# Moving the load of Wo and one activation-table load in a graph-attention and mixture-of-experts layer

## The chip, the cores and the metric

The kernel runs on one core of one Trainium2 chip. A core has five engines that run their own instruction lists: TensorE (PE in the profile; its weight loads are shown apart as PEld), VectorE (DVE), ScalarE (ACT), GpSimd (POOL) and SyncE (SP). They meet only through semaphores. Transfers are issued from the lists of SP, ACT and POOL and carried out by 16 shared DMA engines; an instruction that issues a transfer waits in its engine's list like any other, and what stands behind it waits too. The metric is the time of one launch in microseconds (us), lower is better. The time before the change is 2276.78 us, the median of five runs (2266.71, 2267.69, 2276.78, 2277.61 and 2291.95 us).

## The reference: what is computed

One layer over N = 4096 nodes with 512 features, in two halves, each with a layer norm ahead of it and a residual around it.

- **Attention over a sparse graph.** For 8 heads of width 64, q, k and v are projected from the normed x by Wqs, Wks, Wvs. A node attends only to its neighbours in `adj` (4096 x 4096, zeros and ones, fewer than one in a hundred of them ones, and far more of those at low node numbers) and to itself:

```python
scores = jnp.einsum('hqk,hmk->hqm', q, k) * kd ** (-0.5)
scores = scores + IDENTITY_BIAS * eye - MASK_VAL * (1.0 - adj)
att = jax.nn.softmax(scores, axis=-1)
return jnp.einsum('hqm,hmk,hko->qo', att, v, Wo)
```

- **Mixture of experts.** Each node goes to the two of 8 experts with the highest logits; an expert is 512 -> 512 -> 512 with a gelu, and the two results are added with softmax weights.

## The kernel before, in words

`_fast` is one long function, and the order of the instructions on each engine is the order in which it is written (a manual schedule); the framework adds the waits. It has three stages.

**Stage one: projections and lists (0 to about 456 us).** For 32 tiles of 128 nodes the kernel norms and transposes x, multiplies it by Wk and Wv, and stores a row of keys, values and packed adjacency words per node in the DRAM table `kv_d`. Queries are projected by `project_q(b, p)` for blocks of 512 nodes, in `NP` = 4 pieces p of 128 columns: four matmuls (L600), then a scaled copy by ACT (L605) and a store to `q_d` issued by ACT (L606). Meanwhile other instructions build, for every tile of queries, index lists `idx` of the neighbours that it has to fetch. The stage ends with the four pieces of the last block:

```python
for p in range(NP):
    project_q(NT // TPB - 1, p)
while jobs:
    step()
```

ACT also computes square roots in this stage (L385, norms), with its own activation table.

**Stage two: attention (about 456 to 1720 us).** The work is cut into steps, and steps are grouped in pairs ("duos"). A step takes one or two sets of 128 neighbours, fetched from `kv_d` into one of 24 slots of a ring in SBUF: a tile's own rows by SP (L702), the others by an indirect DMA that POOL issues (L707), whose instruction is visible on POOL as DMA_INDIRECT. For each step, `turn` transposes the keys on PE (L734, tile `pkT`) and has ACT copy them to SBUF (L736, tile `kT`); `scores` multiplies them with the queries (L771, tile `ps`) and has ACT take the exponential (L778, tile `pr`); DVE masks it by the adjacency bits (L784, or L782 for own rows); `values` multiplies by the values (L799). After a query tile's last step its sums are divided, transposed and multiplied by Wo (`project`, L844), which is the only reader of the tile `wo`; the route to the experts follows in the same loop.

**Around the change.** Between the stages stand these lines, in this order (L1118 to L1174, helpers left out):

```python
nc.vector.tensor_copy(wg32[:, :, :E], wg)
tick = small.tile([1, 1], F32, bufs=1, name="tick")
wo = mid.tile([P, NP, D], F32, name="wo")
nc.scalar.dma_start(out=wo, in_=Wo...)        # L1121, 1024 KB, on ACT's queue
...
issue(3, -1)
duo(turn, 0)
nc.gpsimd.tensor_copy(tick, steps[duos[0][0]]["kT"][0][:1, 0, :1])   # L1170
issue(AHEAD, -1)
duo(scores, 0)
duo(turn, 1)
duo(turn, 2)
n = 0
```

`issue(k, n)` issues the fetches of the duos below k. Duos 0 to 2 need one fetch by SP and seven by POOL. The copy `tick` on POOL reads one element of the first `kT`, so no later fetch is issued before that copy is done. `AHEAD` is 5, and inside the loop that follows `issue` goes on as far as the ring has slots, so in POOL's list sixteen more fetches stand behind `tick` ahead of the first one that needs a slot back.

The tile `wo` lies in memory that stage one used. So its load waits, at the head of what ACT has left, for the last stores of stage one, that of the last piece of queries among them. ACT's list at the joint of the stages is: copy of query piece 2 and its store; copy of piece 3 and its store; the load of `wo`; two copies `kT` of duo 0; a table load for the exponential; two exponentials of duo 0; four copies `kT` of duos 1 and 2; exponentials of duo 1; and so on.

**Stage three: experts (about 1720 us to the end)** is not touched by the change.

Of the kernel before, what the change touches and what calls it, by code (L numbers as in the profile page):

```python
# [9 lines left out]
F32 = mybir.dt.float32  # L10
# [4 lines left out]
AF = mybir.ActivationFunctionType  # L15
# [5 lines left out]
P = 128  # L21
# [49 lines left out]
def fast(tc, dram, flag, x, adj, Wks, Wqs, Wvs, Wo, Wg, bg, W1, b1, W2, b2, out):  # L71
    with ExitStack() as ctx:
        _fast(ctx, tc, dram, flag, x, adj, Wks, Wqs, Wvs, Wo, Wg, bg, W1, b1, W2, b2, out)


def _fast(ctx, tc, dram, flag, x, adj, Wks, Wqs, Wvs, Wo, Wg, bg, W1, b1, W2, b2, out):
    nc = tc.nc
    N, D = x.shape
# [7 lines left out]
    NP = H * KD // P  # L86
# [29 lines left out]
    eps = const.tile([P, 1], F32, name="eps")  # L116
    nc.vector.memset(eps, EPS)
    bits = const.tile([P, NW, 16], U16, name="bits")
    for k in range(16):
# [4 lines left out]
        out=below, in_=below, pattern=[[1, P]], compare_op=ALU.is_gt, fill=0.0,  # L124
# [209 lines left out]
    with ExitStack() as s1:  # L334
# [7 lines left out]
        work = s1.enter_context(tc.tile_pool(name="p1", bufs=2))  # L342
# [205 lines left out]
        for h in range(NHC):  # L548
# [4 lines left out]
            g, c = divmod(h, NH)  # L553
# [36 lines left out]
        def step():  # L590
            nonlocal slot
            for f in jobs.pop(slot, []):
                f()
            slot += 1

        def project_q(b, p):
            pq = ps_m.tile([P, TB], F32, tag="mm", name=f"pq_{b}_{p}")
            for c in range(DC):
                step()
                nc.tensor.matmul(  # L600
                    pq, w["q"][:, c, ts(p, P)], xTs[b][:, c, :],
                    start=(c == 0), stop=(c == DC - 1),
                )
            qT = work.tile([P, TB], F32, tag="qT", bufs=3, name=f"qT_{b}_{p}")
            nc.scalar.mul(qT, pq, KD ** -0.5)  # L605
            nc.scalar.dma_start(out=q_d[:, p, ts(b, TB)], in_=qT)  # L606

        for i in range(NT):
            b, t = divmod(i, TPB)
            kvr = kvrs[i % 2]  # L610
            for k, n in enumerate(("k", "v")):
# [15 lines left out]
                out=kv_d[1 + i * P : 1 + (i + 1) * P, :HV], in_=kvr.bitcast(I32)  # L627
# [2 lines left out]
                project_q(b - 1, t)  # L630
        for p in range(NP):
            project_q(NT // TPB - 1, p)
        while jobs:
            step()

# [9 lines left out]
    with ExitStack() as s2:  # L645
# [3 lines left out]
        mid = s2.enter_context(tc.tile_pool(name="mid", bufs=1, side="right"))  # L649
# [223 lines left out]
        def route(g, n):  # L873
# [243 lines left out]
        AHEAD = 5  # L1117
        nc.vector.tensor_copy(wg32[:, :, :E], wg)  # L1118
        tick = small.tile([1, 1], F32, bufs=1, name="tick")
        wo = mid.tile([P, NP, D], F32, name="wo")  # L1120
        nc.scalar.dma_start(  # L1121
            out=wo, in_=Wo.rearrange("h k o -> (h k) o").rearrange("(c p) o -> p c o", p=P)
        )
        issued = 0

        def issue(upto, n):
# [35 lines left out]
        def duo(f, n):  # L1162
            if n < S:
                for s in duos[n]:
                    f(s)
# [6 lines left out]
        duo(scores, 0)  # L1172
        duo(turn, 1)
        duo(turn, 2)  # L1174
        n = 0
        while n < S or any(k >= n for k in later):
            duo(scores, n + 1)
# [86 lines left out]
    with ExitStack() as s4:  # L1264
        work = s4.enter_context(tc.tile_pool(name="p4", bufs=2))
# [793 lines left out]
```

## Time and profile before

| | before |
|---|---|
| median of five runs | 2276.78 us |
| profiled execution, its own time | 2272.34 us |
| its span, first to last instruction | 2270.6 us |
| mean granted TensorE clock | 0.941 of full |
| PE busy | 91% of the span |
| ACT, DVE, POOL busy | 35%, 43%, 25% |
| moved by DMA | 462 MB, mean 203 GB/s |

All of the profile comes from the one profiled execution. A line of the timeline reads: start, duration, engine, line of the kernel, operation, written tile <- read tiles, shapes, how many instructions were merged, and in brackets how long the engine sat idle before it and what ended that wait. "issue" means that the engine waited for nothing that the profile shows. ACTq marks instructions of ACT's list that only issue or wait. A matmul in float32 with these shapes leaves two records. A row of the table by windows reads: stretch, its length, busy time (and records) of PE, PEld, DVE, ACT and POOL, the granted TensorE clock as a share of full speed, the mean busy share of the 16 DMA engines, and what they moved in GB/s.

### The profile page before, as it was taken

What the parts mean: (1) busy time and instruction counts of PE and PEld (TensorE: products, weight loads), DVE (VectorE), ACT (ScalarE), POOL (GpSimd) and SP (SyncE); (2) the same over time, 40 slices, a digit from 0 to 9 for tenths busy, and PEclk for the clock granted to TensorE, in tenths of its full rate; (3) what the DMA queues carried; (4) which work ended last, traced back from release to release, by engine and by line L of the source; (5) the groups of instructions that cost most, each with busy time, mean ns of one, the idle gap of its engine ahead of it and who ended that gap; (6) DMA issues with size and microseconds to landing.
All of it is one profiled execution on the core that took longest, in us unless ns stands there. A gap on an engine that the chain in (4) does not pass through costs nothing. (4 is left out here: it accounts for less than half of the span.)

```text
span 2270.6 us, 59938 instructions
## 1 busy us (share of the span) xinstructions
PE 2056.2 (91%) x25581; PEld 1352.7 (60%) x25581; DVE 971.4 (43%) x2519; ACT 793.5 (35%) x1166; POOL 561.9 (25%) x716
## 2 busy tenths in 40 slices
PE   9899999979999978979979889788887999999997
PEld 4344444468777757767757667576665444444443
DVE  3456655425434434434434445245354333333332
ACT  3233333135444524524534345243431222222221
POOL 2000000143333342343242331423211122222221
PEclk9999999989999989979979889798898999999999
DMA  9778773486677666766667584866686455455532
GB/s 373 255 263 263 261 262 123 156 296 225 222 234 250 227 225 215 228 223 220 221 221 232 175 273 157 274 206 192 220 291 234 106 109 116 107 123 133 110 72 44
DMA packets 193602, 462.00 MB, mean 203 GB/s; under 512 B 30384, under 2 KB 46768, under 8 KB 193200
## 3 DMA queue, kind: packets, MB, share of 16 engines
q0 software_dynamic: 66784, 248.65, 36.1%
q1 hardware_dynamic: 102096, 178.04, 23.7%
q10 hardware_dynamic: 24448, 31.38, 4.1%
q8 instruction: 206, 3.38, 0.6%
q14 instruction: 68, 0.56, 0.1%
HBM read 385.37 MB, written 72.64 MB: 202 GB/s over the span
## 5 line engine op out<-in xcount | busy, mean ns | idle before, releaser
L707 POOL DMA_INDIRECT ring<-kv_d,idx x361 | 355.4, 985 | 1084.2 <-issue 471.1
L771 PE MATMUL ps<-q,kT 64*64 64x64 f32 (+1 forms) x10224 | 398.5, 245 | 106.7 <-issue 93.1
L778 ACT ACTIVATE pr<-ps 128x1024 f32<-128x1024 f32 x270 | 272.4, 1025 | 565.7 <-PE ps L771 431.3
L784 DVE SCALAR_TENSOR_TENSOR pr<-t,pr 128x1024 f32<-128x1024 uint16 x238 | 285.7, 1223 | 402.5 <-ACT pr L778 341.0
L771 PEld LDWEIGHTS ps<-q,kT 64*64 64x64 f32 (+1 forms) x10224 | 327.2, 153 | 186.2 <-issue 163.7
L799 PE MATMUL o<-ring,pr 128*64 128x65 f32 x8640 | 309.2, 228 | 32.3 <-issue 32.3
L799 PEld LDWEIGHTS o<-ring,pr 128*64 128x64 f32 x8640 | 281.5, 141 | 66.0 <-issue 62.8
L734 PE MATMUL pkT<-ident,ring 128*128 128x128 f32 x1572 | 226.8, 295 | 21.1 <-issue 13.2
L1402 PE MATMUL ph<-ring,xT 128*128 (+1 forms) x528 | 238.2, 594 | 0.8 <-ACT xT L1364 0.8
L734 PEld LDWEIGHTS pkT<-ident,ring 128*128 128x128 f32 x1572 | 186.2, 150 | 43.8 <-issue 20.6
L736 ACT COPY kT<-pkT 128x512 f32<-128x512 f32 (+1 forms) x270 | 199.3, 787 | 26.1 <-PE pkT L734 12.5
L1458 POOL DMA_INDIRECT out_dram<-y,r x66 | 101.9, 1544 | 371.1 <-ACT y L1453 284.2
L1431 PE MATMUL py_e<-ring,hT 128*128 (+1 forms) x396 | 182.3, 596 | 1.6 <-ACT hT L1424 1.6
L1402 PEld LDWEIGHTS ph<-ring,xT 128*128 128x128 f32 (+1 forms) x528 | 91.3, 183 | 99.8 <-issue 98.7
L1453 ACT ACTIVATE y<-y,wt 128x512 f32<-128x512 f32 x66 | 47.6, 722 | 269.8 <-DVE y L1449 230.0
L615 PE MATMUL pv<-wv,xT 128*128 128x512 f32 x256 | 130.0, 603 | 0.0
L844 PE MATMUL py<-wo,oT 128*128 128x512 f32 x256 | 125.2, 634 | 2.6 <-ACT part L937 1.8
L615 PE MATMUL pk<-wk,xT 128*128 128x512 f32 x256 | 125.7, 610 | 0.7 <-ACT xT L409 0.7
L600 PE MATMUL pq<-xT,wq 128*128 128x512 f32 x256 | 123.1, 603 | 0.0
L1407 DVE COPY h<-ph 128x512 f32<-128x512 f32 x66 | 45.7, 692 | 169.9 <-PE ph L1402 169.9
L1431 PEld LDWEIGHTS py_e<-ring,hT 128*128 128x128 f32 (+1 forms) x396 | 67.2, 183 | 76.0 <-issue 74.1
L1073 POOL DMA_INDIRECT xs_d<-x,slot_i x58 | 63.8, 1100 | 173.7 <-DVE x L1069 57.1
(281 smaller groups left out, 1905.9 us busy)
## 6 DMA issues: line engine op xcount, KB each, us to landing
adj<-in_adj_dram SPq DMA_DIRECT2D x64, 1024.0 KB
wo<-in_L_ffn_W_dram SPq DMA_DIRECT2D x72, 256.0 KB
kv_d<-kvr ACTq DMA_DIRECT2D x32, 516.0 KB
ring<-kv_d SPq DMA_DIRECT2D x32, 516.0 KB
r<-xs_d SPq DMA_DIRECT2D x57, 258.0 KB
ring<-in_L_ffn_W_dram SPq DMA_DIRECT2D x56, 256.0 KB
xt<-in_x_dram SPq DMA_DIRECT2D x32, 256.0 KB
q_d<-qT ACTq DMA_DIRECT2D x32, 256.0 KB
```

Of the source, the lines that this page charges most:

```text
L600: nc.tensor.matmul(pq, w["q"][:, c, ts(p, P)], xTs[b][:, c, :], start=(c == 0), stop=(c == DC - 1),)
L615: nc.tensor.matmul(pk, xTs[b][:, c, ts(t, P)], w[n][:, c, :], start=(c == 0), stop=(c == DC - 1),)
L707: nc.gpsimd.indirect_dma_start(out=g, out_offset=None, in_=kv_d, in_offset=bass.IndirectOffsetOnAxis(ap=idx[i // GL][:, i % GL, a : a + 1] ...
L734: nc.tensor.transpose(pk[:, x * NP + p, :], g[:, ts(p, P)], ident)
L736: nc.scalar.copy(kT[:, : nk * NP], pk[:, : nk * NP])
L771: nc.tensor.matmul(ps[c : c + nk, r, p * P + x * nq : p * P + (x + 1) * nq], kT[r * KD : (r + 1) * KD, p, c : c + nk], q[r * KD : (r + 1) ...
L778: nc.scalar.activation(pr.rearrange("p h q -> p (h q)"), ps.rearrange("p r f -> p (r f)"), AF.Exp)
L784: nc.vector.scalar_tensor_tensor(pr, st["t"].unsqueeze(1).to_broadcast([P, H, P]), 0.0, pr, op0=ALU.is_gt, op1=ALU.mult,)
L799: nc.tensor.matmul(o[c * HALF : (c + 1) * HALF, h // NP, (h % NP) * VW : (h % NP + 1) * VW], pr[:, hd * NP + p, c * HALF : (c + 1) * HALF] ...
L844: nc.tensor.matmul(hold["py"], hold["oT"][:, c, :], wo[:, c, :], start=(c == 0), stop=(c == NP - 1),)
L1402: nc.tensor.matmul(ph[a], xTs[b][:, c, a], w, start=(c == 0), stop=(c == DC - 1), skip_group_check=b >= FULL,)
L1431: nc.tensor.matmul(py[a], hTs[b][:, c, a], w, start=(c == 0), stop=(c == HC - 1), skip_group_check=b >= FULL,)
```

## The change

Two edits. The tile `wo` and its load are written after the scores of duo 0 and the transposes of duos 1 and 2, in place of ahead of everything in stage two. And after piece 2 of the last block of queries ACT takes the exponential of one column of a constant into a tile of its own, `one`, that nothing reads; the table load for the exponential then stands there.

```diff
         for p in range(NP):
             project_q(NT // TPB - 1, p)
+            if p == NP - 2:
+                one = work.tile([P, 1], F32, tag="one", name="one")
+                nc.scalar.activation(one, eps, AF.Exp)
         while jobs:
             step()
...
         tick = small.tile([1, 1], F32, bufs=1, name="tick")
-        wo = mid.tile([P, NP, D], F32, name="wo")
-        nc.scalar.dma_start(
-            out=wo, in_=Wo.rearrange("h k o -> (h k) o").rearrange("(c p) o -> p c o", p=P)
-        )
         issued = 0
...
         duo(scores, 0)
         duo(turn, 1)
         duo(turn, 2)
+        wo = mid.tile([P, NP, D], F32, name="wo")
+        nc.scalar.dma_start(
+            out=wo, in_=Wo.rearrange("h k o -> (h k) o").rearrange("(c p) o -> p c o", p=P)
+        )
         n = 0
```

In the changed kernel ACT's list at the joint is: copy of query piece 2 and its store; the table load and the exponential `one`; copy of piece 3 and its store; two copies `kT` of duo 0; two exponentials of duo 0; four copies `kT` of duos 1 and 2; the load of `wo`; exponentials of duo 1. The lists of PE, DVE, POOL and SP are the same as before, with the same waits.

## The prediction

> **What bounds the kernel now.** I read the page's first part, then busy times by stage, then the timelines of ACT, PE and POOL around the joint of stages one and two, the only place that the diff touches.
>
> ```profile
> PE 2056.2 (91%) x25581; PEld 1352.7 (60%) x25581; DVE 971.4 (43%) x2519; ACT 793.5 (35%) x1166; POOL 561.9 (25%) x716
> ```
>
> ```profile
> 0.00:455.00 455.00, 436.82 (x2474) 204.79 (x2474) 236.74 (x721) 139.40 (x304) 19.61 (x126) 0.99 0.72 245
> 455.00:488.00 33.00, 19.85 (x187) 16.23 (x188) 7.11 (x16) 11.24 (x14) 16.36 (x17) 0.70 0.90 346
> 488.00:1720.00 1232.00, 1072.10 (x21135) 877.83 (x21134) 542.05 (x1326) 519.78 (x648) 409.31 (x496) 0.91 0.68 226
> ```
>
> PE is the busy engine of every long stage (96% and 87% above). The joint, 455 to 488 us, is the exception: PE is busy for 19.85 of 33 us, at a mean clock of 0.70. ACT's timeline shows why it begins late:
>
> ```profile
> 451.94 0.33 ACTq L606 DMA_DIRECT2D q_d<-qT  x1
> 455.27 0.60 ACT L605 ACTIVATE qT<-pq 128x512 f32<-128x512 f32 x1 [3.36 <-PE pq L600]
> 455.90 0.33 ACTq L606 DMA_DIRECT2D q_d<-qT  x1
> 459.14 0.39 ACTq L1121 DMA_DIRECT2D wo<-in_L_gnn_Wo_dram  x1
> 459.62 1.07 ACT L736 COPY kT<-pkT 128x512 f32<-128x512 f32 x2 [3.76 <-DMA q_d<-qT]
> 460.72 1.28 ACT L778 ACT_TABLE_LOAD   x1
> 462.01 1.02 ACT L778 ACTIVATE pr<-ps 128x1024 f32<-128x1024 f32 x1
> 463.38 1.02 ACT L778 ACTIVATE pr<-ps 128x1024 f32<-128x1024 f32 x1 [0.35 <-PE ps L771]
> ```
>
> The last store of queries is issued at 455.90. The load of Wo behind it can be issued only when that store has landed, at 459.14, and the first copies of turned keys stand behind the load. PE and POOL wait for those copies:
>
> ```profile
> 455.97 1.07 PE L734 MATMUL pkT<-ident,ring 128*128 128x128 f32 x8 [0.73 <-issue]
> 460.26 3.07 PE L771 MATMUL ps<-q,kT 64*128 64x128 f32 x32 [3.23 <-ACT kT L736]
> 463.27 3.43 PE L734 MATMUL pkT<-ident,ring 128*128 128x128 f32 x24
> 466.62 1.08 PE L771 MATMUL ps<-q,kT 64*64 64x64 f32 x38
> ...
> 483.76 2.72 PE L734 MATMUL pkT<-ident,ring 128*128 128x128 f32 x12 [0.64 <-issue]
> ```
>
> ```profile
> 460.27 0.18 POOL L1170 COPY tick<-kT 1x1 f32<-1x1 f32 x1 [11.51 <-ACT kT L736]
> 460.61 0.96 POOL L707 DMA_INDIRECT ring<-kv_d,idx  x1 [0.16 <-issue]
> ```
>
> PE turned the keys at 455.97 and stood still for 3.23 us. Then comes a second, larger loss that the change does not address: from 467.5 to 483.1 PE gets through only the last 42 of the 80 records of duo 1's scores, in bursts of one to six with gaps marked "issue". These 15.6 us lie inside POOL's burst of sixteen fetches behind `tick`, 460.6 to 481.4, with the DMA engines full:
>
> ```profile
> 458.00:460.00 2.00, 0.00 (x0) 0.00 (x0) 0.00 (x0) 0.38 (x1) 0.00 (x0) 1.00 0.02 6
> 462.00:464.00 2.00, 2.00 (x18) 1.77 (x15) 0.93 (x1) 1.64 (x2) 1.70 (x2) 0.50 1.10 398
> 470.00:484.00 14.00, 6.05 (x29) 4.28 (x30) 0.00 (x0) 0.09 (x1) 8.62 (x10) 0.55 1.02 406
> ```
>
> The same sight returns in every later place where POOL issues back to back: around 810 us PE's `values` trickle from 809.7 while POOL issues from 805.2, and run again at 823.7, when POOL pauses. So I take it that this stretch ends with POOL's burst, whatever PE has left.
>
> **The change, part by part.** (1) The load leaves the head of ACT's list. Nothing then stands between the store at 455.90 and the first `kT`, whose waits are on PE and DVE alone. Its four transposes, the first half of the x8 row, end at 456.60; the copy then starts at about 456.65 in place of 459.62: 2.97 us earlier. `tick`, the burst and the first scores each hang on that copy by fixed steps (460.27 minus 459.62 is 0.65; 460.26 minus 459.62 is 0.64), so all move by 2.97.
>
> (2) PE's clock. The granted share falls to 0.77 and 0.50 in 460 to 464, behind the gap, and the first scores take 3.07 us; the same 32 records take 2.06 us later (at 504.31). Without the gap up to 1.0 us goes, and some 0.2 of the transposes: 0 to 1.2 us more. But it is regained ahead of the trickle, which ends with POOL, so at 2.7 records per us (42 in 15.6) 1.2 us earlier buys 3 records, 0.1 us at full speed. I take 0.1.
>
> (3) The table load, 1.28 us, and the new exponential (nearest row: the one-column square root of L385, 0.29) take 1.57 us between 452.27, when the store's issue ends, and 455.27, when ACT next has work: a hole of 3.00, spare 1.43. Cost nothing; with no cover it would hold the last queries by 1.57. What it frees at 460.72 is at most 0.7 us: at full clock the first half of duo 0's scores is done 1.03 after 457.29, at 458.3, and a load left behind the two `kT` copies would end at 459.0. PE covers that with 24 transposes (3.4 us) before it needs ACT again. I take 0, keep 0 to 0.7.
>
> (4) The load's new place. Its issue, 0.39, follows the four copies of duos 1 and 2 (464.97 plus 2.91, less about 3: near 465), when the stores that it waits for have landed (459.1). Behind it on ACT stand duo 1's exponentials, due after 480: ACT is idle for 16.04 us there. No engine waits; SP and POOL keep their lists. Its data, 1 MB, now fall among the fetches, 2.6 us at 406 GB/s; before, they went ahead of them (the engines moved 218 and 398 GB/s from 460 to 464). The fetches behind it feed duo 3 and later, which PE takes up only at the end of the trickle, and POOL issues every 1.24 us unhindered: cost 0 to 0.6, taken 0. The first reader, L844, comes at 571.1 us, 107 us later.
>
> Sum: 2.97 + 0.1 + 0 + 0 = **3.1 us** off, bounds 2.4 (2.97 less 0.6) to 4.9 (2.97 + 1.2 + 0.7). After the joint no row is tied to the clock on the wall, so the shift reaches the end. The profiled execution took 2272.34 us (2270.6 of span and 1.74 around it): it would take 2269.2. That execution lies 4.4 below the median of the five, 2276.78; a median is what will be compared, so I forecast 2276.78 - 3.1 = **2273.7**.
>
> Two rules of the Trainium skill are weighed here. "ScalarE: Activation LUTs", under "What ACT_TABLE_LOAD costs", adds a drain of about 1.38 us to a load, 2.66 us in all; with 0.29 that would fill 2.95 of the 3.00 us hole, and any slip would delay the last queries. In the row above the next exponential starts 0.01 us after the load, so this trace shows no such drain; by either the sum stays 3.1. "TensorE: Matmul & The Clock Gate", in "Part 1: The HAM clock gate", halves the clock after an idle window of about 3.4 us; read as a gap of that length, the 3.23 us here would cost no clock, and the sum would be 3.0. The trace did halve it.
>
> **The rivals.** *Nothing is kept.* The trickle could end at its old time, if what ends it is the drained transfers and not POOL: the 1 MB that no longer goes ahead, and a store that is still landing, may eat the lead of 2.97. For it: DMA is at 1.02 until 484. Against it: the engines do next to nothing in 458 to 460 (6 GB/s), which the change fills. Time 2276.8.
>
> *Slower.* PE enters the trickle earlier. Before, it ran 94 record pairs of weight load and matmul at full rate from 460.26 to 467.5, out of what its sequencer held when POOL began; 3.23 us of standstill preceded. If less is at hand without that pause, more is left at the burst's end. Worst: the trickle from the start, 20.8 us of burst at 2.7 a us, 56 records of the 136 (32 + 24 + 80) that were done before; 80 remain, 3.0 us at full clock and 6.0 at half. Against 3.0 gained that is 0 to 3 lost: 2280. It turns slower once more than 40 records (3.0 us at the half clock) are left. For it: nothing shows how many were held. Against it: 809.7 is 4.5 us into POOL's burst with no pause ahead of it.
>
> *Larger gain.* PE's supply lasts a little longer and the scores of duo 1 are out before the trickle; then the 12 transposes and 64 records of `values` that now take 483.76 to 489.32 also go early: 3.1 + 5.6, time 2268. For it: the scores start 0.9 us earlier relative to the burst at full clock. Against it: the trickle seems to hang on the count of instructions, which is unchanged.
>
> **How the numbers follow.** Forecast 0.60, nothing kept 0.16, slower 0.12, larger gain 0.12. All lie within 1% (22.8 us), about what a measurement of this kernel can tell from no change: its five runs span 25.2 us, so even a median may stray some 7 us. The range takes in the rivals and part of that: 2268 - 6 = 2262 to 2280 + 5 = 2285. Faster or slower by over 1% has only this scatter behind it: 0.03 each, 0.94 the same.
>
> **What would show it.** Right: the first `kT` directly behind the last store's issue, PE's gap before the first scores under 0.5 us, clock at 1.00 in them, `tick` near 457.3, the table load near 452.3, POOL's sixteen fetches ended by 478.5, the second transposes near 480.7. Wrong: a wait on the last store again, fewer than 38 records before the trickle, or another length of it.

## The result and the profile after

The changed kernel takes 2274.48 us (median of 52 runs), the kernel before 2276.52 us (94 runs): ratio **0.999, 95% interval 0.998 to 1.0001**, or 2.3 us less with an interval from 4.6 less to 0.2 more (the medians differ by 2.0). No difference that the measurement can tell. Ratios leave out runs over 1.5% above the fastest of their kernel, two of the 52 here. The profiled execution after took 2274.75 us (span 2273.0, clock 0.938), 2.4 us more than the one before, although the joint went as intended. ACT's timeline after, in the columns explained above (line numbers are 3 higher than before):

```profile
452.67 1.28 ACT L635 ACT_TABLE_LOAD   x1 [0.39 <-ACT qT L605]
453.96 0.20 ACT L635 ACTIVATE one<-eps 128x1 f32<-128x1 f32 x1
455.64 0.60 ACT L605 ACTIVATE qT<-pq 128x512 f32<-128x512 f32 x1 [1.47 <-PE pq L600]
456.26 0.33 ACTq L606 DMA_DIRECT2D q_d<-qT  x1
457.00 1.07 ACT L739 COPY kT<-pkT 128x512 f32<-128x512 f32 x2 [0.77 <-PE pkT L737]
459.21 1.02 ACT L781 ACTIVATE pr<-ps 128x1024 f32<-128x1024 f32 x1 [1.14 <-PE ps L774]
461.40 1.02 ACT L781 ACTIVATE pr<-ps 128x1024 f32<-128x1024 f32 x1 [1.16 <-PE pkT L737]
...
464.29 0.39 ACTq L1175 DMA_DIRECT2D wo<-in_L_gnn_Wo_dram  x1
...
475.45 1.02 ACT L781 ACTIVATE pr<-ps 128x1024 f32<-128x1024 f32 x1 [10.22 <-remote]
481.86 1.02 ACT L781 ACTIVATE pr<-ps 128x1024 f32<-128x1024 f32 x1 [5.38 <-remote]
```

The table load and the exponential stand in the old hole, and the last copy of queries still waits 1.47 us for PE behind them: nothing was delayed. The first `kT` waits for PE alone. From the start of the last copy of queries it starts after 1.36 us in place of 4.35. PE's and POOL's timelines after:

```profile
456.33 1.07 PE L737 MATMUL pkT<-ident,ring 128*128 128x128 f32 x8 [0.73 <-issue]
457.64 2.06 PE L774 MATMUL ps<-q,kT 64*128 64x128 f32 x32 [0.24 <-ACT kT L739]
459.62 1.53 PE L737 MATMUL pkT<-ident,ring 128*128 128x128 f32 x12
462.48 1.56 PE L737 MATMUL pkT<-ident,ring 128*128 128x128 f32 x12 [1.32 <-ACT pr L781]
463.97 1.04 PE L774 MATMUL ps<-q,kT 64*64 64x64 f32 x52
...
466.79 3.02 PE L774 MATMUL ps<-q,kT 64*64 64x64 f32 x20 [0.37 <-issue]
470.43 1.23 PE L737 MATMUL pkT<-ident,ring 128*128 128x128 f32 x5 [0.62 <-issue]
...
476.53 1.11 PE L737 MATMUL pkT<-ident,ring 128*128 128x128 f32 x4 [3.87 <-issue]
...
481.78 3.17 PE L802 MATMUL o<-ring,pr 128*64 128x65 f32 x53 [0.44 <-issue]
```

```profile
457.65 0.18 POOL L1169 COPY tick<-kT 1x1 f32<-1x1 f32 x1 [8.58 <-ACT kT L739]
457.99 0.96 POOL L710 DMA_INDIRECT ring<-kv_d,idx  x1 [0.16 <-issue]
...
478.84 0.94 POOL L710 DMA_INDIRECT ring<-kv_d,idx  x1 [0.30 <-issue]
```

The page's first line and the row of the joint in the table by windows:

```profile
PE 2056.0 (90%) x25581; PEld 1356.3 (60%) x25581; DVE 972.0 (43%) x2519; ACT 794.0 (35%) x1167; POOL 563.2 (25%) x716
```

```profile
452.00:485.00 33.00, 22.17 (x233) 17.00 (x236) 8.53 (x22) 11.73 (x16) 18.86 (x18) 0.73 0.94 358
```

PE's busy time is as before. At the joint, PE is busy for 22.17 of 33 us in place of 19.85 (the stretch is laid 3 us earlier, as the work is). PE's standstill of 3.23 us is 0.24, and the first scores take 2.06 us in place of 3.07. New is a standstill of 1.32 us after the first twelve transposes. The stretch in which PE gets through only a few records at a time, with gaps marked "issue" (the trickle), is still there, from 465 until 481.78. POOL's run of sixteen fetches, 457.99 to 479.78, begins before it and ends 2.0 us ahead of its end (2.4 us before: 481.4 and 483.76).

In this stretch PE's rows don't tell when its results are ready. By them the scores of duo 1 end at 467.1 and 469.8, but ACT is released to their exponentials only at 475.45 and 481.86. "remote" means that no recorded end lies close to the release: the semaphore that PE raises rose 8.3 and 12.0 us after the recorded ends. Away from POOL's runs it rises 0.02 us after them (median in this trace).

Where did the gain go afterwards? Measured at the products with Wo (L847 after, L844 before), in time from the start of the span, the profile after minus that before is -1.85 us at the first product, -5.80 at the second, +2.58 at the fourth, -2.80 at the 18th and +2.20 at the last: it wanders inside stage two. Stage three takes the same time in both. So the two profiled executions can't show a difference of 3 us at the end; only many runs can, and those put it at 2.3 with the interval above.

### The profile page after: what moved, and what is told of

It is laid out like the page before. It is cut to its first block, busy times and chain, and to the rows that moved or that the text cites. A ratio compares the mean times of both kernels' runs of the same rounds, so it can differ in the third digit from the quotient of the medians.

```text
span 2273.0 us, 59939 instructions
## 1 busy us (share of the span) xinstructions
PE 2056.0 (90%) x25581; PEld 1356.3 (60%) x25581; DVE 972.0 (43%) x2519; ACT 794.0 (35%) x1167; POOL 563.2 (25%) x716
## 5 line engine op out<-in xcount | busy, mean ns | idle before, releaser
L774 PE MATMUL ps<-q,kT 64*64 64x64 f32 (+1 forms) x10224 | 393.5, 246 | 92.0 <-issue 81.7
L847 PE MATMUL py<-wo,oT 128*128 128x512 f32 x256 | 123.5, 627 | 2.9 <-ACT part L940 1.7
L1076 POOL DMA_INDIRECT xs_d<-x,slot_i x58 | 65.2, 1125 | 175.3 <-DVE x L1072 57.3
```

The source lines that it names most:

```text
L774: nc.tensor.matmul(ps[c : c + nk, r, p * P + x * nq : p * P + (x + 1) * nq], kT[r * KD : (r + 1) * KD, p, c : c + nk], q[r * KD : (r + 1) ...
L847: nc.tensor.matmul(hold["py"], hold["oT"][:, c, :], wo[:, c, :], start=(c == 0), stop=(c == NP - 1),)
```

## The experiments

A comparison with a time is made with runs of the kernel before on the same chip, and a ratio has its 95% interval. In the landmarks, time is counted from the start of the last copy of queries (the L605 row near 455.5). None of the kernels leaves work out. Those with an addition are named.

### The two edits alone

Without the exponential (the other edit kept):

```diff
-            if p == NP - 2:
-                one = work.tile([P, 1], F32, tag="one", name="one")
-                nc.scalar.activation(one, eps, AF.Exp)
```

> The changed kernel without the early exponential: only the load of Wo is moved. My theory (the wait at the head of ACT's list was the whole cost, the table load is free): the first copy of turned keys starts under 1 us after the last store of queries is issued, PE's gap before the first scores is under 0.5 us, and the table load stands behind the two copies and delays the first exponential by at most 0.7 us, which PE covers with its 24 transposes. Rival (the table load was part of the gain): the first exponential comes over 1 us later than in the changed kernel, relative to the first copy, and PE waits for it.

One run, 2286.69 us, beside a median before of 2293.60 on that chip (2277.13 to 2302.57). Its ACT timeline:

```profile
458.02 1.07 ACT L736 COPY kT<-pkT 128x512 f32<-128x512 f32 x2 [0.77 <-PE pkT L734]
459.11 1.28 ACT L778 ACT_TABLE_LOAD   x1
460.40 1.03 ACT L778 ACTIVATE pr<-ps 128x1024 f32<-128x1024 f32 x1
461.79 1.02 ACT L778 ACTIVATE pr<-ps 128x1024 f32<-128x1024 f32 x1 [0.36 <-PE pkT L734]
```

The first `kT` is at +1.36 us as in the changed kernel. The table load stands behind it again, and the first exponential starts at +3.75, against +3.57 and +3.21 in two executions of the changed kernel. The second one, released by PE, starts at +5.14, against +5.76 and +5.77. In this trace the early exponential frees nothing that PE needs.

The kernel before with the exponential, Wo still ahead:

```diff
+            if p == NP - 2:
+                one = work.tile([P, 1], F32, tag="one", name="one")
+                nc.scalar.activation(one, eps, AF.Exp)
```

> The kernel before with the early exponential alone. My theory: the first copy of turned keys still waits for the landing of the last store of queries, about 3.7 us on ACT, and PE stands still about 3.2 us before the first scores; the clock still falls behind the gap. Only the 1.28 us table load is gone from between the copies and the first exponential, and that exponential then waits for PE instead, at most 0.3 us earlier. Rival (the table load was a real part): the joint is shorter by about 1.3 us.

One run, 2291.59 us. Its ACT timeline:

```profile
460.55 0.39 ACTq L1124 DMA_DIRECT2D wo<-in_L_gnn_Wo_dram  x1
461.03 1.07 ACT L739 COPY kT<-pkT 128x512 f32<-128x512 f32 x2 [2.97 <-DMA q_d<-qT]
```

The wait on the store is there, so the load of Wo is what holds the first `kT`. But `kT` starts at +3.56, not at +4.35: here the load is issued 2.45 us after the issue of the last store, in the profile before 3.24 us after it. The price of the wait is not a constant; in two executions the first `kT` came 2.99 and 2.20 us behind the +1.36 without it.

### Is a delay at the joint carried to the end?

The changed kernel with 48 exponentials of 128 x 256 on ACT ahead of the first `kT`; they write junk into a tile that is filled later:

```diff
         AHEAD = 5
+        for _ in range(48):
+            nc.scalar.activation(
+                inverses.rearrange("p i h -> p (i h)"), blank[:, : NT * H], AF.Exp
+            )
```

> The changed kernel with 48 exponentials of 128x256 on ACT between the last store of queries and the first copy of turned keys, so that the first copy comes some 15 to 22 us later (the trace gives the exact delay). My theory: no row behind the joint is tied to absolute time, so the whole delay reaches the end, within the scatter of stage two: time of the changed kernel plus the delay. Rival (a shift at the joint is absorbed by slack in stage two): less than half of the delay is left at the end.

The first `kT` starts at +22.36 us, 21.0 later than in the changed kernel. ACT's timeline of this run:

```profile
457.62 21.45 ACT L1122 ACTIVATE inverses<-blank 128x256 f32<-128x256 f32 x48 [0.40 <-ACT qT L605]
478.98 1.05 ACT L739 COPY kT<-pkT 128x512 f32<-128x512 f32 x2
```

Time 2308.64 us, ratio to before 1.0083 (1.0048 to 1.0118), which is 19.0 us (11.0 to 27.1) over the kernel before; 21.0 less the 2.3 that the changed kernel gains is 18.7. So more than half of the delay reaches the end, and within the interval all of it; at the first product with Wo (+137.25) all of it is there. That a gain of 2 to 3 us at the joint reaches the end in the same way is likely, but not shown: the interval is wider than the gain.

### The changed kernel again

No edit; it shows how far two executions of one program differ.

> The changed kernel itself, beside the others of this group on one chip, as their baseline. My theory: 1 to 4 us under the kernel before; first copy of turned keys 1.4 us after the last copy of queries starts, values of duo 0 ended 28 to 32 us after it (before: 34.1). Rival (nothing is kept): same time as before to within 1 us.

2274.11 us (12 runs), ratio 1.0002 (0.9978 to 1.0026). Its joint agrees with the profile after up to the trickle and then differs: by PE's rows the scores of duo 1 end at +27.54 us in place of +14.17. By ACT's, the last exponential of duo 1 starts at +27.59 in place of +26.22. Side by side with the two kernels and the two single edits, in us from the last copy of queries:

| run | Wo moved | first kT | scores of duo 1 end by PE's rows | ACT's last exponential of duo 1 | values of duo 0 end | values of duo 7 end | first product with Wo |
|---|---|---|---|---|---|---|---|
| before | no | 4.35 | 27.86 | 29.56 | 34.12 | 75.24 | 115.81 |
| exponential only | no | 3.56 | 22.00 | 28.80 | 33.40 | 77.17 | 117.89 |
| after | yes | 1.36 | 14.17 | 26.22 | 29.32 | 73.02 | 113.60 |
| after again | yes | 1.36 | 27.54 | 27.59 | 31.73 | 74.53 | 115.07 |
| Wo only | yes | 1.36 | 22.78 | 26.79 | 31.73 | 74.04 | 114.73 |

The row of ACT before, where both exponentials of duo 1 are merged:

```profile
483.91 1.94 ACT L778 ACTIVATE pr<-ps 128x1024 f32<-128x1024 f32 x2 [16.04 <-PE ps L771]
```

PE's rows put the end of duo 1's scores 13 us apart in two executions of the same program, ACT's row puts it 1.4 us apart, and both are out of the joint within 1.5 us of each other. ACT's last exponential of duo 1 starts 2.1 to 5.1 us behind the end of POOL's run in all five. The first product with Wo comes at 114.5 in the mean of the three with Wo moved and at 116.9 in that of the two without: 2.4 us, the size of the wait removed (2.2 to 3.0). With three and two executions that differ by 1.5 and 2.1 us among themselves, this is weak evidence by itself.

### What the trickle is: POOL's run of fetches, or full DMA engines?

The changed kernel with a gate on POOL, for the first eight passes of the loop: the copy `tick` reads the first `kT` of duo n + 3 before the next fetches are issued.

```diff
         AHEAD = 5
+        GATED = 8
...
+                if n < GATED:
+                    nc.gpsimd.tensor_copy(
+                        tick, steps[duos[n + 3][0]]["kT"][0][:1, 0, :1]
+                    )
                 issue(n + 1 + AHEAD, n)
```

> The changed kernel with a one-element copy on POOL, reading the newest turned keys, ahead of each of the next eight groups of fetches, so that POOL issues two fetches per duo in place of sixteen back to back. My theory (PE trickles because POOL issues fetches back to back): the stretch of bursts with gaps marked issue between about 465 and 482 us shrinks to a few us behind the first five fetches, the values of duo 0 end near 473 in place of 485, and the time falls by about 10 us, to 2264. Rival (PE's supply stalls there for another reason, or the later fetches then come late): the stretch stays over 10 us, or PE waits for fetched rows instead, and the time is within 3 us of the changed kernel.

2287.84 us, ratio 0.9978 (0.9952 to 1.0003). The 10 us expected did not come. But the trickle at the joint is gone: the scores of duo 1 end at +11.55, ACT's last exponential of duo 1 starts at +11.60, and the values of duo 7 end at +58.12, 14.9 us ahead of the changed kernel. When the gate is lifted POOL catches up, with sixteen fetches on end from 515.65 to 537.45, and PE trickles there. PE's timeline of this run:

```profile
463.53 0.75 PE L774 MATMUL ps<-q,kT 64*64 64x64 f32 x28
464.71 1.91 PE L774 MATMUL ps<-q,kT 64*64 64x64 f32 x52 [0.43 <-issue]
466.56 1.53 PE L737 MATMUL pkT<-ident,ring 128*128 128x128 f32 x12
468.02 2.09 PE L802 MATMUL o<-ring,pr 128*64 128x65 f32 x64
...
531.49 0.82 PE L774 MATMUL ps<-q,kT 64*128 64x128 f32 x4 [0.61 <-issue]
```

The first product with Wo comes at +117.06, 3.5 us later than in the changed kernel. The trickle goes where POOL's run goes.

The other way round, the changed kernel without the holding copy, so that POOL issues all 23 fetches from 440.73 to 471.04, over the end of stage one:

```diff
         duo(turn, 0)
-        nc.gpsimd.tensor_copy(tick, steps[duos[0][0]]["kT"][0][:1, 0, :1])
         issue(AHEAD, -1)
```

> The changed kernel without the copy on POOL that holds the sixteen fetches until the first turned keys are copied: POOL issues all 23 from 440 us on, beside the last projections of queries, and is done near 470 in place of 480. My theory (the trickle lasts as long as POOL's run of fetches, and the projections, with few long matmuls, do not suffer from it): the trickle ends near 471 to 473, the values of duo 0 end 18 to 22 us after the last copy of queries starts in place of 29, and the time falls by 7 to 10 us against the changed kernel. Rival (PE has to lose a fixed amount, or the first seven fetches and the last stores of queries then land late): first transposes come later by several us, or the trickle covers the same count of records, and the time stays within 3 us.

2275.87 us (median of all 12), ratio 0.9981 (0.9951 to 1.0011): the 7 to 10 us expected did not come. PE's timeline:

```profile
452.15 3.60 PE L600 MATMUL pq<-xT,wq 128*128 128x512 f32 x8
471.76 1.94 PE L737 MATMUL pkT<-ident,ring 128*128 128x128 f32 x8 [16.02 <-issue]
473.89 3.13 PE L774 MATMUL ps<-q,kT 64*128 64x128 f32 x32 [0.19 <-ACT kT L739]
```

Now PE's rows show one block of 16.02 us ahead of the first transposes, marked "issue" like the gaps of the trickle, and it ends 0.72 us behind POOL's last fetch. The last projections of queries, recorded as done by 455.75, reach ACT late as well: its last two copies of queries start at 460.51 and 471.07, both "remote", in place of about 452 and 456. Then PE goes on without a trickle; its first values end at 485.5 us, as in the profile after (485.0). Moved earlier, the loss is as large as before.

Full DMA engines without POOL: the gate again, and behind `tick` (by a copy of 4 bytes that waits for it) SP copies 8.4 MB from DRAM to DRAM.

```diff
+        full = dram.tile([1, GL * P, N], F32, name="full_d")
...
+            nc.sync.dma_start(
+                out=full[k], in_=adj[k * GL * P : (k + 1) * GL * P, :N]
+            )
         issue(AHEAD, -1)
...
```

> The gated kernel with one copy of 8.4 MB from DRAM to DRAM, issued by SP when POOL's holding copy is done, so that the transfer engines are full behind the first scores while POOL issues few fetches. My theory (POOL's run of fetches makes the trickle, full transfer engines alone do not): PE runs duos 1 to 4 without long runs of gaps marked issue, though it may wait for rows that land late, and the busy share of the transfer engines is above 0.9 there. Rival (full transfer engines make the trickle): bursts of one to six records with gaps marked issue over 10 us or more, with POOL idle in between.

One run, 2286.43 us. Its table by windows, then PE's timeline:

```profile
464.00:470.00 6.00, 3.21 (x87) 2.61 (x84) 3.57 (x9) 4.00 (x5) 1.15 (x1) 0.96 0.98 371
470.00:482.00 12.00, 0.07 (x1) 0.10 (x2) 0.26 (x2) 0.00 (x0) 0.00 (x0) 0.50 1.11 373
```

```profile
465.72 1.90 PE L774 MATMUL ps<-q,kT 64*64 64x64 f32 x51 [0.41 <-issue]
481.93 1.09 PE L737 MATMUL pkT<-ident,ring 128*128 128x128 f32 x4 [14.31 <-DMA ring<-kv_d,idx]
```

With the engines at 0.98 and POOL at one fetch, duo 1's scores run at full speed; then PE waits 14.31 us for fetched rows, and the wait is named. So here full engines give a named wait on data, and a run of POOL's fetches gives short bursts of PE with gaps named "issue". PE had only some 3 us of work in that stretch, but two other traces say the same of the fetched rows themselves: without the holding copy the engines are at 1.02 from 472 to 476 us, still with POOL's rows but POOL no longer issuing, and PE is busy for 3.81 of the 4 us; before, they are at 1.01 from 484 to 486, and PE is busy throughout.

How POOL's issuing reaches into PE stays open. A late fetch of PE's instructions is not what the traces show: they list the transfers of instructions, and PE goes on without one. In the profile before none starts between 463.98 and 484.63 us, and PE goes on at 483.76; without the holding copy none starts between 444.05 and 477.53, and PE goes on at 471.76.

The gate through all of stage two:

```diff
         AHEAD = 5
+        GATED = S - 3
...
+                if n < GATED:
+                    nc.gpsimd.tensor_copy(
+                        tick, steps[duos[n + 3][0]]["kT"][0][:1, 0, :1]
+                    )
                 issue(n + 1 + AHEAD, n)
```

> The one-element copies on POOL of the gated kernel, kept up through the whole of stage two, so that the fetches are never more than about three duos ahead. In the gated kernel the trickle went from 464-482 us, and a run of 17 fetches came back at 515-537 us when the gate was lifted. My theory (a run of fetches back to back is what costs, and every gate lift or long wait of POOL makes one): without a lift there is no second trickle at 523-538, the first product with Wo comes 12 to 15 us earlier than in the changed kernel, and the time falls by 5 to 20 us, unless POOL's waits for its scatters then leave PE waiting for rows. Rival (the deep lead is needed): PE waits for fetched rows at each scatter, several us at every group of four tiles, and the time is above the kernel before.

2322.16 us, ratio 1.0216 (1.0165 to 1.0267): slower, where 5 to 20 us less were expected. It has no run of eight fetches before 1725 us, yet PE's busy time rose to 2095.5 us from 2056.0, and its waits on `pr` (PE `pkT` <- ACT `pr`) to 20.3 us from 10.2. Why its matmuls take longer was not settled. So doing away with the runs is not enough by itself, and what follows is only that a short lead, held by a gate, is no cure.

### A lead that grows, and where its gain came from

If the loss comes with runs, the lead can be built up slowly: in pass n POOL issues the fetches of the duos below n + 6 + n/3, over the first 18 duos, with the gate; behind them the lead stays at n + 12.

```diff
+                if n < 18:
+                    nc.gpsimd.tensor_copy(
+                        tick, steps[duos[n + 3][0]]["kT"][0][:1, 0, :1]
+                    )
-                issue(n + 1 + AHEAD, n)
+                issue(n + 1 + AHEAD + min(n, 18) // 3, n)
```

> As after, but for the first 18 duos POOL issues only as far ahead as a lead that grows by one duo every three duos: in each of these loop passes POOL's copy `tick` first reads the first kT of duo n+3 and POOL then issues the fetches of the duos below n + 6 + n/3 (whole number), so that neither sixteen fetches at the start nor a catching-up burst later stand back to back. Nothing is left out. Theory 1 (PE loses time only where POOL issues in a long run, and the loss is more than one fetch costs when it stands alone): no trickle at 464 to 482 us, none near 515 to 540, first L844 product about 104 to 110 us after the last copy of queries in place of 113.6 to 115.1, time 5 to 10 us below that of the changed kernel, ratio to the kernel before 0.994 to 0.997. Theory 2 (each fetch costs PE about the same wherever it stands, so the loss is only spread): first L844 at 113 to 117, ratio 0.998 to 1.001. Theory 3 (the smaller lead lets late rows through, as when the gate stood through all of stage two): named waits of PE on fetched rows or of POOL on kT grow, time up to 15 us above.

The same over 12 duos, with n/2:

```diff
+                if n < 12:
+                    nc.gpsimd.tensor_copy(
+                        tick, steps[duos[n + 3][0]]["kT"][0][:1, 0, :1]
+                    )
-                issue(n + 1 + AHEAD, n)
+                issue(n + 1 + AHEAD + min(n, 12) // 2, n)
```

> The same with a lead that grows by one duo every two duos over the first 12. Theory 1: the lead is rebuilt at twice the pace at which one fetch per step is needed, so a milder trickle than in the changed kernel is left: first L844 about 107 to 112 us after the last copy of queries, time 2 to 7 us below the changed kernel, ratio 0.995 to 0.998. Theory 2: 113 to 117, ratio 0.998 to 1.001. Theory 3: up to 10 us above, less than with the slower ramp.

2258.35 us, ratio **0.9906** (0.9874 to 0.9938), and 2261.72 us, ratio **0.9914** (0.9881 to 0.9947). Both are faster than the kernel before, and by more than the largest gain expected of them. But not by the mechanism expected: the first product with Wo comes at +110.21 us in the slow ramp (expected 104 to 110) and at +120.91 in the quick one (expected 107 to 112), which is later than in the changed kernel. Nor did the ramps do away with the runs: POOL still issues fifteen fetches on end from 520.79 to 543.65 in the slow one and eleven from 534.07 to 549.97 in the quick one. Most of the gain must lie behind that product. In the profile after, POOL's timeline at one of six like places:

```profile
1262.00 0.09 POOL L1075 MEMSET tick<- 1x1 f32 x1
1283.19 3.07 POOL L1076 DMA_INDIRECT xs_d<-x,slot_i  x1 [21.11 <-DVE x L1072]
...
1287.87 0.98 POOL L710 DMA_INDIRECT ring<-kv_d,idx  x1 [0.30 <-issue]
```

L1076 scatters rows of x to the experts, and POOL's list holds fetches behind it. POOL waits 21.11 us for the scatter's data and then issues eighteen transfers, scatters and fetches, in a run, and PE trickles: it is busy for all 21 us from 1262 to 1283, while POOL waits, and for 13.08 of the 25 us from 1283 to 1308. The same stands at 808, 998, 1147, 1418 and 1580 us, with waits of 11.6 to 21.1 us. With a lead of n + 12, nine, ten, seven, nine, eight and four more fetches stand ahead of the first scatter of each group, POOL has work until the data are there, and all six waits are gone in both ramps (at most 1.9 us is left of one). That made two explanations, told apart by doing either half alone.

The deep lead without gate and ramp:

```diff
-                issue(n + 1 + AHEAD, n)
+                issue(n + 1 + AHEAD + 6, n)
```

> As after, but in the loop POOL's list goes on to the fetches of the duos below n + 12 in place of n + 6, as far as the ring has slots; no added copies on POOL, the run of sixteen at the start stays. Nothing is left out. It undoes the first half of the kernel with the slow ramp and keeps its second. Theory A (that kernel gained 23 us over the changed one, by its trace, not at the start but because nine, ten, seven, nine, eight and four more fetches then stand ahead of the first scatter of each group of tiles, so that POOL no longer waits 12 to 21 us at that scatter with fetches behind it and then issues 13 to 18 of them in a run): the trickle at 464 to 482 stays, first L844 product 113.6 to 116 us after the last copy of queries, the six waits at scatters gone, time 14 to 22 us below the kernel before, ratio 0.990 to 0.994. Theory B (the gain came from the ramp at the start): ratio 0.998 to 1.001, the waits at the scatters still there or gone without effect.

2270.28 us, ratio **0.9924** (0.9897 to 0.9951), with the trickle at the joint kept (first product with Wo at +114.17). POOL's timeline of this kernel where the changed one waited 21.11 us:

```profile
1300.57 0.94 POOL L710 DMA_INDIRECT ring<-kv_d,idx  x1 [4.55 <-DVE pr L787]
1301.52 0.09 POOL L1075 MEMSET tick<- 1x1 f32 x1
1301.82 1.01 POOL L1076 DMA_INDIRECT xs_d<-x,slot_i  x1 [0.21 <-POOL tick L1075]
```

The groups of POOL by line (busy us, mean ns of one, idle us ahead), the scatters after and then here; the idle time falls by 92.9 us, and the six waits were 96.0 together:

```profile
L1076 POOL DMA_INDIRECT xs_d<-x,slot_i x58 | 65.2, 1125 | 175.3 <-DVE x L1072 57.3 <-DVE var L884 56.1 <-ACT pr L781 26.8
```

```profile
L1076 POOL DMA_INDIRECT xs_d<-x,slot_i x58 | 62.5, 1077 | 82.4 <-DVE var L884 55.3 <-DVE place L1001 11.5 <-issue 10.4
```

The table by windows at three of the six places, of after and then of this kernel:

```profile
1140.00:1174.00 34.00, 19.82 (x362) 16.62 (x359) 8.64 (x29) 8.75 (x10) 18.07 (x24) 0.70 0.68 234
1278.00:1312.00 34.00, 20.07 (x332) 16.12 (x332) 8.70 (x27) 8.44 (x11) 20.49 (x26) 0.67 0.64 226
1410.00:1446.00 36.00, 21.25 (x377) 17.34 (x374) 9.98 (x35) 8.62 (x11) 20.51 (x25) 0.73 0.68 231
```

```profile
1140.00:1174.00 34.00, 30.12 (x717) 24.38 (x716) 18.73 (x57) 14.44 (x18) 15.58 (x15) 0.99 0.75 250
1278.00:1312.00 34.00, 30.28 (x592) 24.70 (x591) 17.70 (x48) 14.59 (x19) 10.80 (x14) 0.95 0.68 226
1410.00:1446.00 36.00, 32.80 (x692) 26.69 (x692) 18.46 (x52) 14.93 (x19) 15.05 (x20) 1.00 0.79 270
```

In these stretches PE gets through almost twice as many records, at a clock of 0.95 to 1.00 in place of 0.67 to 0.73: the clock is low where PE trickles. Over the whole trace PE's gaps named "issue" ahead of scores, values and transposes of keys fall from 141.2 to 120.6 us. A deep lead also brings every row in earlier; a kernel that moves only the fetches at the six scatters was not tried, so the share of the waits in the gain is argued from these traces. The other half, the ramp and then the old lead of n + 6:

```diff
+                if n < 18:
+                    nc.gpsimd.tensor_copy(
+                        tick, steps[duos[n + 3][0]]["kT"][0][:1, 0, :1]
+                    )
-                issue(n + 1 + AHEAD, n)
+                issue(n + 1 + AHEAD + (n // 3 if n < 18 else 0), n)
```

> The other half: the slow ramp of the first 18 duos with its copies on POOL, and after it the lead of n + 6 again as in the changed kernel, so that each scatter stands behind the same fetches as there. Nothing is left out. Theory A: no trickle at 464 to 482, first L844 product about 110 us after the last copy of queries, 3 to 5 us ahead of the changed kernel, and no more than that at the end, since the six waits and runs at the scatters are back: ratio 0.996 to 0.999. Theory B: ratio 0.990 to 0.993 as with the whole of it.

2285.87 us, ratio 0.9992 (0.9965 to 1.0019). The trickle at the joint is gone (values of duo 7 end at +59.14), but the lead of 13.9 us is lost by the first product with Wo (+113.83, expected about 110), and the six waits are back. (In this kernel, too, POOL still issues twelve fetches on end, from 516.88 to 534.06.) So the gain of the ramps is that of the deep lead. The traces say it again in two halves, cut where the 4321st of the 8640 records of `values` starts, counted from the last copy of queries:

| run | first half, us | from there to the end, us |
|---|---|---|
| before | 594.5 | 1220.8 |
| after | 592.6 | 1224.8 |
| after again | 597.9 | 1219.9 |
| ramp, then old lead | 588.1 | 1226.9 |
| deep lead | 607.6 | 1204.0 |
| slow ramp, deep lead | 592.1 | 1201.8 |
| quick ramp, deep lead | 610.2 | 1195.0 |

The second half is 1195 to 1204 us with the deep lead and 1220 to 1227 without it. In the first half the two kernels that build the deep lead quickly are 10 to 18 us longer than the changed kernel, and the slow ramp is not longer; these are single executions, and by their ratios the three kernels with a deep lead can't be told apart. A deep lead that sets in only after the first half was not tried.

## Why the prediction was right

The forecast was 2273.7 us, in a range of 2262 to 2285; the measured 2274.5 lies 0.8 above it. Its sum, 3.1 us, lies within the measured 2.3 (4.6 less to 0.2 more). So size and sign are compatible with it, and the interval just includes nothing at all. The time by itself says little: a forecast of no change (2276.8) would have lain in the range too, and that it is met to 0.8 us is partly luck, because the median of five runs, from which it starts, could stray by 7 us and was 0.3 off. What speaks for the prediction is the joint.

- **(1) The load off ACT's head: right.** First `kT` moved by 2.99 us against the last copy of queries (2.97 expected); `tick` and the first scores moved with it. The exponential-only run shows the price of the wait to vary with the landing of the store, 2.20 and 2.99, so the 2.97 taken from one execution was the upper of the two.
- **(2) The clock: the sum was right, the way there wrong.** The first scores took 2.06 us at a clock of 1.00 (457 to 460 us), 1.0 less, and the 24 transposes 3.09 in place of 3.43. But PE did not cover the exponentials with these transposes: after twelve of them it stood still for 1.32 us, until ACT's second exponential was done (1.33 us in the repeat). So nothing of the clock's gain was left even at the joint: the scores of duo 1 start 8.34 us after the last copy of queries in place of 11.35, 3.0 earlier. The term of 0.1 came out by a loss that the prediction did not have. The clock falls after shorter gaps too: in the exponential-only run PE's gap was 2.44 us, and the clock 0.76 and then 0.50 from 462 to 466.
- **(3) The table load: right that it costs nothing and gains nothing.** 1.28 and 0.20 us in the hole, 1.47 us of wait left behind it (spare expected 1.43), and nothing gained downstream, as the Wo-only run shows. The next ACTIVATE started 0.01 us after the load, so here too no drain was seen behind it. That PE needs ACT only after 24 transposes was wrong, see (2).
- **(4) The load's new place: right where it could be seen.** It was issued at 464.29, without a wait. A cost of its data among the fetches was not measured apart.
- **The trickle: right in what sets its end, wrong in its detail.** That it belongs to POOL's run is shown by moving the run later and earlier, and the last exponential of duo 1 follows the end of the run by 2.1 to 5.1 us in five executions. But "2.7 records per us" counts PE's rows, and these do not tell when results are ready: by them duo 1's scores ended 13 us apart in two executions of the changed kernel, by ACT's 1.4 us apart. (The row of 38 ends at 467.70, not 467.5, which hardly changes the rate; and the 94 pairs ahead of the trickle had a clock of 0.50 to 0.88 from 460 to 466 us, not the full rate.) PE's rows turn keys from 470.43, not from 480.7. POOL's run took 21.8 us, not 20.8, and ended at 479.8, not by 478.5. The run lasts 20.2 to 21.8 us across the traces, so its length scatters by 1.6 us, about half of the 3 us.
- **The shift reaches the end: not contradicted, not shown.** The delay of 21.0 us arrived as 19.0 (11.0 to 27.1) over the kernel before; for 3 us the interval is too wide. One pair of traces can't show such a shift, because single executions wander by several us in stage two: between the second and the fourth product with Wo the profile after loses 8.4 us on the one before. This lies between 626 and 732 us, ahead of the first scatter at 808, so the runs behind the scatters did not make it; what did is open.

The "nothing kept" rival is not what the joint shows: 2.4 us were still there at the first product with Wo, in the means of the five executions of the table. At the end the interval doesn't quite exclude it. The "slower" rival did not come, but part of what it describes did: the standstill of 1.32 us lies in POOL's run, after 44 records, where before 94 passed without a gap. Even so PE got 84 records of scores out (32 and 52) before the first gap named "issue", against 70 before (32 and 38). The "larger gain" rival saw PE's rows of duo 1's scores end early, at 469.8, in one of two executions; ACT got these scores only at 475.45 and 481.86. The values of duo 0 ended 4.8 us earlier than before by the last copy of queries, 2.4 in the repeat, and no gain of 8.7 us was left at the first product with Wo. How much PE's sequencer had at hand is still not known.

## What to carry to other kernels

When a list has a transfer whose data are late, look at what stands behind it: through POOL's wait of 21 us PE stayed busy, but in the run of fetches that followed it did half its work, and a lead deep enough to put fetches ahead of that wait gave 0.8%. Gaps of an engine named "issue" belong to no wait in the table; line them up in time with the other engines' runs, and look at when the next engine is released before you take the end of a row for the end of the work. And a wait seen in one trace is one draw of its price: before sizing a gain by it, see what it is in a second execution.

## What the runs showed of the hardware

- While POOL issues indirect fetches back to back, most of them 0.94 us each with 0.30 between, PE gets through a few records at a time with gaps marked "issue" (42 in 15.4 us before, or none in 16.02 us without the holding copy). A pair of fetches leaves two or three gaps: in the kernel with the slow ramp, fetches at 469.90 and 471.17 us, and PE's gaps of 0.24, 0.36 and 0.36 us between 470.96 and 472.65. DMA engines at a share of 0.98 to 1.02 with POOL not issuing did not do it.
- In such a run the release of the next engine can come long after the end of PE's row: 8.3 and 12.0 us for the scores of duo 1 in the profile after, against a median of 0.02 us away from the runs.
- The clock follows PE's activity: the mean clock was 0.67 to 0.73 in the stretches with a run at 1140 to 1446 us and 0.95 to 1.00 in the same stretches without one.
- An instruction that waits for the store of queries was released 2.45 us after that store's issue in one execution and 3.24 us in another.
